# Images 19 to 31 of an iterated matrix square root: the square is turned by VectorE and DMAs, where TensorE transposed v

## The chip, the cores and the metric

The kernel runs on one core of a Trainium2 chip. The metric is the device time of one execution in microseconds (us). TensorE (PE in the profile; its weight loads are PEld) multiplies matrices from SBUF into PSUM. VectorE (DVE) and ScalarE (ACT) read and write PSUM and SBUF; GpSimd (POOL) works on SBUF alone. SyncE (SP) computes nothing and issues DMAs; ACT can issue DMAs too. Each engine takes its instructions in order.

## The reference

Input x is 32 images of 32 channels of 128x128 float32. Layer 0 adds to each channel the approximate square root of its normalised self:

```
x = x + _L0_conv_ref(_gn(x))         # _gn: mean and variance over pairs of channels
  # _L0_conv_ref, for each of the 1024 matrices A2 (128x128):
  normA = jnp.sqrt(jnp.sum(A2 * A2, axis=(1, 2)))
  Y = A2 / normA;  Z = I
  for _ in range(5):
      T = 0.5 * (3.0 * I - jnp.matmul(Z, Y))
      Y = jnp.matmul(Y, T)
      Z = jnp.matmul(T, Z)
  sA = Y * jnp.sqrt(normA)
x = x + _L1_conv_ref(_gn(x), weights1, weights2)
  # a 2-D Fourier transform of each channel, 2 x 32 x 32 low modes multiplied by a
  # 32x32 channel matrix each, and the transform back
```

## The kernel before

**Tiles.** The work of layer 0 is cut into 256 groups of four channels (8 groups to an image). A group's tiles are 128 partitions by 4 x 128 float32 (256 KB). `products(lhsT, rhs)` is four matmuls into one PSUM bank, `lhsT` transposed times `rhs` for each channel; TensorE records two instructions for each float32 product of 128 columns, and one for a transpose. `m` holds the matrices in one orientation, `mb` (loaded as `b`) in the other, since `lhsT` must come transposed.

**One group** is one call of `newton` (line 462). Five steps of the iteration are folded into two polynomials of degree four ("quartics") and a last step. There are two forms. Images 1 to 18 are "far" (`is_far`, line 357): `far_quartic` (line 442). Image 0 and images 19 to 31 are "near": `near_quartic` (line 407). The near form:

- TensorE makes the square, `products(mb, m)`; VectorE adds a multiple of m from SBUF and writes `v`.
- GpSimd makes `r = mb + eye` (a 128x512 TENSOR_TENSOR).
- TensorE transposes `v` (four transposes through PSUM); VectorE adds `r` and writes `w`.
- TensorE makes `products(v, w)`; VectorE adds the scaled identity and writes `q`.

The second quartic of a group runs on a new `m` (ScalarE's copy of a product) and on `mb`, its transpose, which TensorE makes and ScalarE copies (`taken(transposed(m), "mb", more)`).

The far form has no such transposes. VectorE turns the square block by block straight out of PSUM (`turned`, 32x32 blocks within each set of 32 partitions); two DMAs on the sync engine carry the result to DRAM (`away`) and back in another order of blocks (`back`), and `by_rows` reads it as the transposed square.

**Staging.** Before a group starts, `fetch` (line 366) loads its two inputs, and `staged` (line 375) normalises them. In near groups GpSimd does all four channels of `m` (four 128x128 TENSOR_SCALAR) and ScalarE the four of `mb`. In far groups ScalarE does two of the four of `m`, and GpSimd also makes a first `v` from `eye_v - mb`. The loads of far groups are issued by the sync engine, those of near groups by ScalarE.

**Order.** The program is written out by hand, as generators. In each "round" every group under way (a "lane") does one step, up to its next `yield`; `rest` is two yields. A near group starts every five rounds (`NEAR = 25 / 5`), a far group every three. A near group lives for some 22 rounds, so that four to five are in flight. Between the lanes' steps the loop at line 1115 places the steps of everything else: statistics of coming images (`prep`), the tail of a finished group (`settle`: store to DRAM, folds on GpSimd, statistics), the forward transform, the mode products and the inverse transform (`inverse`, line 953). The inverse of images 0 to 19 runs beside the groups of the later images. It loads `yt` and `ob` and stores `out` on the sync engine (512 KB each for yt and out) and has GpSimd add `d` to `yt`. Engines and queues keep exactly this order. The transfers that SP and ACT issue take eight semaphores in turn, so that each waits until the one that last used its semaphore has landed.

**Buffers.** `rooms` (line 308) gives the tags of four-channel tiles their numbers of buffers: the first number lasts for the whole run, the second is for `early` tiles, which are there only until `MORE` groups are done.

Of the kernel before, what the change touches and what calls it, by code (L numbers as in the profile page):

```python
# [36 lines left out]
P = 128  # L37
# [56 lines left out]
def conv_preact_kernel(  # L94
# [127 lines left out]
    def prep(bs, made):  # L222

        n = len(bs)
        nc_, ng = n * C, n * G
        first_b = bs[0]
        st = small.tile([P, ng, 6], F32, tag="a_st", name=f"a_st{first_b}", bufs=2)
        tiles = []
        parts = [(b, i) for b in bs for i in range(C // 4)]

        ahead = 3 if first_b else 8

        def load(k):
# [12 lines left out]
        for k in range(len(parts)):  # L246
            for j in range(2):
                nc.vector.bn_stats(st[:, 2 * k + j, :], tiles[k][:, j, :])
            yield
            if k + ahead < len(parts):  # L250
                load(k + ahead)
        ms = small.tile([P, ng], F32, tag="a_ms", name=f"a_ms{first_b}")
        nm, d = yield from moments(st, ms, "a")
        yield from pause
        pq = bank()[:, 0, 0:nc_]
        nc.tensor.matmul(pq, avg_mean, d.rearrange("p g c -> p (g c)"), start=True, stop=True)
        if not first_b:
# [26 lines left out]
        off = off.rearrange("p g c -> p (g c)")  # L284
        sn = small.tile([P, nc_], F32, tag="a_t_s", name=f"a_t_s{first_b}", bufs=3)
        for k, b in enumerate(bs):
            g, c = slice(k * G, k * G + G), slice(k * C, k * C + C)
            made[b] = (nm[:, g], sc[:, c], off[:, c], sn[:, c])
        yield
        nn = small.tile([P, ng, 2], F32, tag="a_d", name=f"a_n{first_b}")  # L290
        nc.vector.tensor_tensor(
            nn,
            s[:, 0:nc_].rearrange("p (g c) -> p g c", c=2),
            iv[:, nc_:, None].to_broadcast([P, ng, 2]),
            ALU.mult,
        )
        nn = nn.rearrange("p g c -> p (g c)")
        for far in sorted({is_far(b) for b in bs}):
            of = [k for k, b in enumerate(bs) if is_far(b) == far]
            c = slice(of[0] * C, of[-1] * C + C)  # L300
            f = EYE_Q * QS if far else EYE * QF
            nc.vector.tensor_scalar_mul(nn[:, c], nn[:, c], P * (1.5 / f) ** 2)
        yield
        yield from root(nn, nc_, sn)
        yield


    rooms = dict(b=(4, 6), xt=(10, 5), x=(3, 2), r=(4, 0), v=(3, 2), w=(3, 2), q=(4, 2))
    rooms.update(my=(4, 3), mb=(2, 4), t=(3, 2), y4=(2, 2), turn=(0, 4))
    turns = dict.fromkeys(rooms, 0)  # L310

    def four(tag, more):
# [8 lines left out]
    def taken(ps, tag, more, f=1.0):  # L321
        t = four(tag, more)
        if f == 1.0:
            nc.scalar.copy(t, ps)
        else:
            nc.scalar.mul(t, ps, f)
        return t
# [12 lines left out]
    def minus(eye, m, t):  # L340

        nc.gpsimd.tensor_tensor(t, eye, m, ALU.subtract)
        return t
# [13 lines left out]
    def is_far(b):  # L357
        return 0 < b < FIRST

    def has_more(b, g):  # L360

        return b * (C // 4) + g < MORE
# [1 line left out]
    raw = {}  # L364

    def fetch(b, g):
        queue = nc.sync if is_far(b) else nc.scalar
        xt, t = four("xt", has_more(b, g)), four("b", has_more(b, g))
        kept(queue.dma_start(out=t, in_=x[b, :, 4 * g : 4 * g + 4, :]))
        kept(queue.dma_start(out=xt, in_=xt_in[b, :, 4 * g : 4 * g + 4, :]))  # L370
        raw[b, g] = xt, t
# [3 lines left out]
    def staged(b, g, nm, sc, off, sn):  # L375

        m = four("x", has_more(b, g))
        xt, mb = raw.pop((b, g))

        def on_scalar(t, x, offset, scale, c):  # L380
            c = slice(c, c + 1)
            kept(
                nc.scalar.activation(t, x, AF.Identity, bias=offset[:, c], scale=scale[:, c])
            )

        for j in range(4):
            c = 4 * g + j
            if j < 2 or not is_far(b):
                kept(
                    nc.gpsimd.tensor_scalar(  # L390
                        m[:, j, :],
                        xt[:, j, :],
                        nm[:, c // 2 : c // 2 + 1],
                        sc[:, c : c + 1],
                        ALU.add,
                        ALU.mult,
                    )
                )
            else:
                on_scalar(m[:, j, :], xt[:, j, :], off, sc, c)  # L400
            on_scalar(mb[:, j, :], mb[:, j, :], off, sc, c)
            yield
        v = minus(eye_v, mb, four("v", True)) if is_far(b) else None
        ready.append((xt, m, mb, v))
        yield

# [32 lines left out]
    def by_rows(t):  # L439
        return blocks(t).rearrange("p a c j -> p c a j")  # L440

    def far_quartic(m, mb, v, f, later, more):

        ps = products(m, mb)
        held = away(turned(ps, more))
        if later:
            yield
        nc.vector.scalar_tensor_tensor(v, ps, 1 / (9 * MS), v, ALU.mult, ALU.add)
        if not later:
            yield  # L450
        minus(eye_q, m, m)
        yield
        w = back(held, "w", more)
        yield
        yield from rest
        q = plus(products(v, by_rows(w)), 9 / (39 * MS**2 * f**2), m, "q", more)
        yield from rest
        return q

    rest = (None, None)  # L460

    def newton(g, sn, xt, m, mb, v, far, more):


        qf, et, eye_t = (QS, EYE_Q, eye_q) if far else (QF, EYE, eye)
        if far:
            q = yield from far_quartic(m, mb, v, 1.0, False, more)
        else:
            q = yield from near_quartic(m, mb, more)
        my = four("my", more)  # L470
# [23 lines left out]
        else:  # L494
            nc.scalar.mul(m, ps, MS / qf)
            yield from rest
            mb = taken(transposed(m), "mb", more)
            yield from rest
            q = yield from near_quartic(m, mb, more)
            both = [bank().rearrange("p (j k) x -> p j k x", k=2) for _ in range(2)]  # L500
            for j in range(4):
                nc.tensor.matmul(both[j // 2][:, j % 2], q[:, j], my[:, j], start=True, stop=True)
# [612 lines left out]
    while todo or any(lanes) or posts or specs or prods or backs:  # L1115
# [3 lines left out]
        for i in range(LANES):  # L1119
# [5 lines left out]
            if lanes[i] is None and todo and room and rounds >= due:  # L1125
                due = max(due, rounds - 1) + (FAR if far else NEAR)
                while norms:
                    step(norms)
                b, g = todo.pop(0)
                xt = ready[0][0]  # L1130
                lanes[i] = (b, g, xt, newton(g, made[b][3], *ready.pop(0), far, has_more(b, g)))
                if stages:
                    stage()
                if not todo:
                    loads.append(weights())
# [88 lines left out]
```

## Time and profile before

| | |
|---|---|
| median of 3 runs | 2981.98 us (2980.7 to 2986.93) |
| profiled execution: time, span | 2981.79 us, 2980.0 us |
| mean granted TensorE clock in it | 0.988 |
| TensorE matmul / weight load busy | 2849.7 us (96%) / 2663.8 us (89%) |
| VectorE / ScalarE / GpSimd busy | 77% / 52% / 67% |
| DMA | 711.90 MB, mean 239 GB/s |

The span runs from the first instruction to the last. A line of the costliest groups names the engine and the operation, the tile written and those read, their shapes, the count, the busy time and the mean of one, and then the engine's idle time just before these instructions with what ended it. A row of a table by stage gives, for a stretch of the span, its length, then the busy time (and count) of PE, PEld, DVE, ACT and POOL, the granted clock, the mean share of time in which the 16 DMA engines were busy, and GB/s. All instructions carry line 88, where a helper records them, so tiles tell them apart. Far groups run from about 30 us to 1560 us, near groups of images 19 to 31 from 1541 us to 2912 us.

### The profile page before, as it was taken

The page shows a single profiled execution, that of the slowest core. Times are in us where ns is not written, and L with a number is a line of the kernel's source. Part 1 is how long each engine was busy: PE and PEld are TensorE (multiplying, and loading weights), DVE is VectorE, ACT ScalarE, POOL GpSimd, SP SyncE. Part 2 cuts the span into 40 slices and gives each one's busy share as a digit, 9 for nine tenths or more (in the row PEclk, how much of TensorE's full clock was granted, in tenths as well). Part 3 has the DMA queues.
Part 4 walks back from the last instruction along what each step waited for, and adds up shares of the span by engine and source line. Part 5 has one row for each costly group of instructions (what it writes and reads, how often), then busy time and mean ns, then how long its engine had stood idle before and what let it go on. Part 6 is the DMA issues. An engine that isn't in the chain of part 4 may idle for free.

```text
span 2980.0 us, 73661 instructions
## 1 busy us (share of the span) xinstructions
PE 2849.7 (96%) x27688; PEld 2663.8 (89%) x27688; DVE 2285.7 (77%) x4407; ACT 1541.3 (52%) x3899; POOL 1988.4 (67%) x2308
## 2 busy tenths in 40 slices
PE   7999999999999999999999999999999999999995
PEld 7899999999999899999999888888888899888983
DVE  7878898889788888888876545886876876777665
ACT  4555555555555555555544445545555544655452
POOL 4667767777777767767755534777777763678452
PEclk9999999999999999999999999999999999999997
DMA  5688889888888889898943566867877737666567
GB/s 177 199 280 272 253 267 281 275 266 282 269 275 257 283 253 294 253 291 255 303 139 104 157 203 208 284 231 242 281 242 248 261 124 226 209 230 218 186 211 268
DMA packets 566897, 711.90 MB, mean 239 GB/s; under 512 B 94736, under 2 KB 329232, under 8 KB 566544
## 3 DMA queue, kind: packets, MB, share of 16 engines
q1 hardware_dynamic: 494400, 574.26, 59.9%
q10 hardware_dynamic: 72144, 132.94, 13.7%
q8 instruction: 221, 3.62, 0.5%
q14 instruction: 132, 1.08, 0.1%
HBM read 440.17 MB, written 266.86 MB: 237 GB/s over the span
## 4 chain that ended last, share of the span: by engine, by line
PE 72%; DMA 12%; DVE 9%; issue 2%; POOL 2%; ACT 1%; SPq 1%; ACTq 0%; DVEq 0%; POOLq 0%
PE ps L88 72%; DMA xs<-in_xs 3%; DMA w<-turn 3%; DVE yt L88 1%; DVE turn L88 1%; DMA turn<-turn 1%; DVE b_d L88 1%; DMA yt<-mid 1%; DMA ob<-od 1%; DVE a_st L88 1%; DVE root L88 1%; DVE q L88 1%; DVE b_st L88 1%; SPq L88 1%; DVE v L88 1%
## 5 line engine op out<-in xcount | busy, mean ns | idle before, releaser
L88 POOL TENSOR_TENSOR fold<-xt 128x256 f32<-128x256 f32 x512 | 364.1, 734 | 308.4 <-DVE xt L88 274.2
L88 ACT ACTIVATE b<-b,a_off,a_sc 128x128 f32<-128x128 f32 x1024 | 467.2, 492 | 127.2 <-issue 27.9
L88 ACT ACTIVATE my<-ps 128x512 f32<-128x512 f32 x512 | 302.4, 602 | 410.4 <-PE ps L88 278.0
L88 PE MATMUL ps<-my,q 128*128 128x128 f32 (+1 forms) x2944 | 475.9, 309 | 6.5 <-ACT my L88 6.4
L88 POOL TENSOR_TENSOR yt<-yt,d 128x512 f32<-128x512 f32 x244 | 306.6, 1283 | 212.3 <-ACT d L88 192.8
L88 PEld LDWEIGHTS ps<-my,q 128*128 128x128 f32 x2944 | 411.9, 191 | 35.4 <-ACT my L88 7.6
L88 PE MATMUL ps<-w,v 128*128 128x128 f32 x2944 | 399.2, 279 | 26.1 <-DMA w<-turn 11.9
L88 POOL TENSOR_TENSOR v<-eye_v,b 128x512 f32<-128x512 f32 x144 | 184.0, 1278 | 352.2 <-ACT b L88 316.2
L88 ACT ACTIVATE t<-ps 128x256 f32<-128x256 f32 (+1 forms) x368 | 171.1, 467 | 462.8 <-PE ps L88 447.2
L88 PEld LDWEIGHTS ps<-w,v 128*128 128x128 f32 x2944 | 362.2, 193 | 41.7 <-issue 10.5
L88 POOL TENSOR_SCALAR x<-xt,a_nm,a_sc 128x128 f32<-128x128 f32 x736 | 323.7, 456 | 15.3 <-DVE a_sc L88 15.0
L88 DVE STREAM_TRANSPOSE turn<-ps 128x512 f32<-128x512 f32 x432 | 295.4, 698 | 45.3 <-PE ps L88 36.9
L88 ACT ACTIVATE y<-ps,a_t_s 128x128 f32<-128x128 f32 x1024 | 292.2, 372 | 42.9 <-PE ps L88 42.7
L88 PE MATMUL ps<-q,t 128*128 128x128 f32 x2048 | 273.4, 277 | 1.3 <-DVE r L88 1.3
L88 PEld LDWEIGHTS ps<-q,t 128*128 128x128 f32 x2048 | 249.0, 192 | 4.2 <-DVE r L88 1.5
L88 DVE BATCH_NORM_STATS2 a_st<-xs 128x6 f32<-128x256 f32 x504 | 184.9, 409 | 77.9 <-DMA xs<-in_xs 77.5
L88 DVE SCALAR_TENSOR_TENSOR w<-ps,r 128x512 f32<-128x512 f32 x224 | 152.9, 683 | 108.7 <-PE ps L88 75.3
L88 DVE SCALAR_TENSOR_TENSOR q<-ps,eye 128x512 f32<-128x512 f32 x224 | 153.3, 684 | 94.2 <-PE ps L88 90.1
L88 DVE TENSOR_TENSOR xt<-ps,xt 128x512 f32<-128x512 f32 x256 | 174.4, 681 | 50.6 <-PE ps L88 48.2
L88 POOL TENSOR_TENSOR r<-mb,eye 128x512 f32<-128x512 f32 x112 | 143.1, 1278 | 86.3 <-ACT mb L88 86.3
L88 DVE TENSOR_TENSOR yt<-ps,yt 128x512 f32<-128x512 f32 x256 | 163.0, 681 | 46.5 <-PE ps L88 40.9
L88 DVE BATCH_NORM_STATS2 b_st<-xt 128x6 f32<-128x256 f32 x512 | 188.0, 407 | 0.5
(147 smaller groups left out, 6296.5 us busy)
## 6 DMA issues: line engine op xcount, KB each, us to landing
turn<-turn SPq DMA_DIRECT2D x432, 256.0 KB
w<-turn SPq DMA_DIRECT2D x288, 256.0 KB
mid<-xt SPq DMA_DIRECT2D x256, 256.0 KB
yt<-mid SPq DMA_DIRECT2D x128, 512.0 KB
xs<-in_xs ACTq DMA_DIRECT2D x252, 256.0 KB
out<-yt SPq DMA_DIRECT2D x115, 512.0 KB
b<-in_x SPq DMA_DIRECT2D x144, 256.0 KB
xt<-in_xt SPq DMA_DIRECT2D x144, 256.0 KB
```

The source lines that it names most:

```text
L88: return self.tc.keep_in_program_order(issue(*args, **kw))
```

## The change

It concerns images 19 to 31 ("late": `b >= FIRST`, 104 groups, 208 quartics).

- `late_quartic` takes the place of `near_quartic`. The square `products(mb, m)` is turned out of PSUM by VectorE (`turned`, as in the far form). `across` then moves it straight to another SBUF tile `w` by four DMAs on the sync engine: each takes 32 partitions and writes 128 partitions by 128 columns (64 KB in pieces of 512 bytes). VectorE adds the square to a `v` that already holds `eye_v - m`. GpSimd turns `mb` into `eye_q - mb` in place. The second product is `products(v, by_rows(w))`, and VectorE adds the new `mb`. The transposes of `v` on TensorE, `r = mb + eye` and the addition of `r` are gone.
- The yields of the new quartic stand at the same distances as in the near one: the second product comes four steps after the first.
- For late groups GpSimd makes `eye_v - m`, once in `staged` (tag `v`) and once in `newton` (tag `r`), and two of the four channels of `m` in `staged` go to ScalarE.
- The loads of late groups (`fetch`) are issued by the sync engine. Image 0 stays on ScalarE.
- `rooms` is dealt anew: `q` 3 and 3 (4 and 2 before), `t` 2 and 3 (3 and 2), `turn` 2 and 2 (0 and 4).
- The scale factors follow (`prep`, `newton`).

```diff
-    rooms = dict(b=(4, 6), xt=(10, 5), x=(3, 2), r=(4, 0), v=(3, 2), w=(3, 2), q=(4, 2))
-    rooms.update(my=(4, 3), mb=(2, 4), t=(3, 2), y4=(2, 2), turn=(0, 4))
+    rooms = dict(b=(4, 6), xt=(10, 5), x=(3, 2), r=(4, 0), v=(3, 2), w=(3, 2), q=(3, 3))
+    rooms.update(my=(4, 3), mb=(2, 4), t=(2, 3), y4=(2, 2), turn=(2, 2))
...
+    def is_late(b):
+        return b >= FIRST
...
-        queue = nc.sync if is_far(b) else nc.scalar
+        queue = nc.sync if b else nc.scalar
...
-            if j < 2 or not is_far(b):
+            if j < 2 or not b:
...
-        v = minus(eye_v, mb, four("v", True)) if is_far(b) else None
+        v = minus(eye_v, mb if is_far(b) else m, four("v", has_more(b, g))) if b else None
...
+    def across(t, more):
+
+        w = four("w", more)
+        for a in range(4):
+            src = t[32 * a : 32 * a + 32].rearrange("p c x -> p (c x)")
+            kept(
+                nc.sync.dma_start(
+                    out=w.rearrange("p c x -> p (c x)")[:, P * a : P * a + P],
+                    in_=src.rearrange("p (b x) -> p b x", b=4),
+                )
+            )
+        return w
+
+    def late_quartic(m, mb, v, more):
+
+        ps = products(mb, m)
+        w = across(turned(ps, more), more)
+        nc.vector.scalar_tensor_tensor(v, ps, 1 / (9 * MS), v, ALU.mult, ALU.add)
+        yield
+        minus(eye_q, mb, mb)
+        yield
+        yield from rest
+        q = plus(products(v, by_rows(w)), 9 / (39 * MS**2), mb, "q", more)
+        yield from rest
+        return q
...
+        elif late:
+            q = yield from late_quartic(m, mb, v, more)
...
             mb = taken(transposed(m), "mb", more)
+            v = minus(eye_v, m, four("r", more)) if late else None
             yield from rest
-            q = yield from near_quartic(m, mb, more)
+            if late:
+                q = yield from late_quartic(m, mb, v, more)
+            else:
+                q = yield from near_quartic(m, mb, more)
```

More of the change, by code (lines that the diff above doesn't have):

```diff
@@ L297, in prep @@
         nn = nn.rearrange("p g c -> p (g c)")
[L298 to L302, printed above, removed]
+        f = EYE_Q * QS if first_b else EYE * QF
+        nc.vector.tensor_scalar_mul(nn, nn, P * (1.5 / f) ** 2)
         yield
@@ L460, in conv_preact_kernel, with newton @@
     rest = (None, None)
-    def newton(g, sn, xt, m, mb, v, far, more):
-        qf, et, eye_t = (QS, EYE_Q, eye_q) if far else (QF, EYE, eye)
+    def newton(g, sn, xt, m, mb, v, far, late, more):
+        qf, et, eye_t = (QS, EYE_Q, eye_q) if far or late else (QF, EYE, eye)
         if far:
             q = yield from far_quartic(m, mb, v, 1.0, False, more)
+        elif late:
+            q = yield from late_quartic(m, mb, v, more)
         else:
@@ L1130, in conv_preact_kernel @@
                 xt = ready[0][0]
-                lanes[i] = (b, g, xt, newton(g, made[b][3], *ready.pop(0), far, has_more(b, g)))
+                lanes[i] = (b, g, xt, newton(g, made[b][3], *ready.pop(0), far, is_late(b), has_more(b, g)))
                 if stages:
```

## The prediction

> **What bounds the kernel now.** I read the page's busy times and slices first: does one engine carry the whole span, or stages in turn?
>
> ```profile
> PE 2849.7 (96%) x27688; PEld 2663.8 (89%) x27688; DVE 2285.7 (77%) x4407; ACT 1541.3 (52%) x3899; POOL 1988.4 (67%) x2308
> PE   7999999999999999999999999999999999999995
> POOL 4667767777777767767755534777777763678452
> DMA  5688889888888889898943566867877737666567
> PE ps L88 72%; DMA xs<-in_xs 3%; DMA w<-turn 3%; DVE yt L88 1%; DVE turn L88 1%; DMA turn<-turn 1%; DVE b_d L88 1%; DMA yt<-mid 1%; DMA ob<-od 1%; DVE a_st L88 1%; DVE root L88 1%; DVE q L88 1%; DVE b_st L88 1%; SPq L88 1%; DVE v L88 1%
> ```
>
> TensorE bounds it from end to end, and the chain that ends last is PE for 72%. The change touches the last stage of groups alone, so I split that by what runs beside it (columns: stretch, length, busy PE, PEld, DVE, ACT, POOL, clock, DMA share, GB/s).
>
> ```profile
> 200.00:1400.00 1200.00, 1172.17 (x10611) 1132.57 (x10611) 1020.15 (x2002) 647.16 (x1662) 881.32 (x976) 1.00 0.86 272
> 1541.00:1700.00 159.00, 154.23 (x1405) 145.83 (x1407) 100.86 (x204) 74.95 (x190) 81.35 (x112) 0.99 0.37 116
> 1700.00:1890.00 190.00, 182.27 (x2161) 163.33 (x2152) 104.58 (x202) 91.05 (x222) 84.89 (x111) 1.00 0.69 218
> 1890.00:2400.00 510.00, 489.19 (x4330) 441.83 (x4330) 399.45 (x734) 267.12 (x703) 398.05 (x458) 0.99 0.73 250
> 2600.00:2720.00 120.00, 116.10 (x1020) 105.17 (x1013) 89.93 (x155) 71.60 (x168) 95.03 (x109) 0.97 0.71 236
> ```
>
> The first row is far groups, which turn by VectorE and DMA already: PE 98% busy with the DMA engines at 0.86. In the late stretches PE is busy 1319.7 of 1371 us. From 1890 to 2400 and from 2600 to 2720 the inverse runs beside the groups, and GpSimd stands at 78% and 79%; elsewhere it is at 45 to 57%. The prices come from the groups by form in 1541 to 2912:
>
> ```profile
> L88 POOL TENSOR_SCALAR x<-xt,a_nm,a_sc 128x128 f32<-128x128 f32 x396 | 172.9, 457 | 0.0
> L88 DVE SCALAR_TENSOR_TENSOR w<-ps,r 128x512 f32<-128x512 f32 x204 | 139.4, 683 | 105.0 <-PE ps L88 72.8 <-POOL r L88 19.7 <-POOL x L88 10.7
> L88 POOL TENSOR_TENSOR r<-mb,eye 128x512 f32<-128x512 f32 x103 | 131.6, 1277 | 72.4 <-ACT mb L88 72.4
> L88 PE MATMUL ps<-ident,v 128*128 128x128 f32 x816 | 126.3, 278 | 5.2 <-DVE v L88 2.6 <-DVE b_mq L88 2.5
> ```
>
> and from TensorE's order of time, where starts can be subtracted, and the waits of PE among far groups:
>
> ```profile
> 2026.78 0.60 PE L88 MATMUL ps<-ident,v 128*128 128x128 f32 x4
> 2027.21 0.60 PE L88 MATMUL ps<-ident,my 128*128 128x128 f32 x4
> 2027.65 1.06 PE L88 MATMUL ps<-x,b 128*128 128x128 f32 x8
> ```
> ```profile
> PE ps L88 <- DMA w<-turn: 15.7, 16, 3.2
> ```
>
> **Transposes of v.** 104 groups x 2 quartics x 4 = 832 leave TensorE. Their duration, 278 ns, is that of overlapping work; what one takes from the next is start to start, (2027.21 - 2026.78)/4 = 0.109 us. Nothing else can use that time in a stretch where PE is the bound: 832 x 0.109 = 91 us. The other end is the row's busy time, 126.3/816 x 832 = 129 us, too high because neighbouring groups share it. I take -91. The products that stay cost the same: far products that read through `by_rows` (w and v, four pieces of 32 columns) start 112 ns apart in the trace, like the plain ones.
>
> **The turned square's way to TensorE.** This is a new wait, and the order gives it four rounds. PE stands in order behind it: if `w` is late, `products(v, by_rows(w))` holds up the four other groups and the inverse. I measured the room in the trace of before. In 1890 to 2400 VectorE starts on the square 1.8 us (median) after its first matmul; at the same place it would now run the block transpose (0.70 us; 698 ns in the page). From the end of that to the products that read `w` there are 8.8 us at the median, 7.8 at the lower quartile, 6.0 in the lowest twentieth; fewer transposes between take some 0.7 us off. In that room go four issues (0.37 us each on SP, as `w<-turn` of far groups) and the landing. The nearest transfer there is `mid<-xt`, same queue, 256 KB: by its packets it ends 3.0 us after its issue at the median, 6.1 at the upper quartile, 6.8 in the worst tenth, since 512 KB loads and stores stand ahead of it. So the last of the four, issued 1.2 us after the block transpose, lands after 4 to 5 us of 8.1 usually, and after about 8 in the worst tenth. One set in six or so comes late, by 1 to 1.5 us: 0.2 us per set. SP itself is no obstacle in before: its last DMA ahead of each set's place had gone out before the block transpose would end, but for 0.3 us in a few stretches. Low end: far groups, 15.7 us over 122 groups x 2 sets = 0.064 us per set, or 13 us for 208 sets. High end: 0.9 us per set, 190 us, if landings move by 3 us because the shared queue holds eight more transfers per group and each DMA waits for the one eight before it. Between them I take 0.19 us per set, +40 us, nearer to far groups, whose DMA engines are busier (0.86) than these will be.
>
> That last number: q1's price in far groups is 77.3% of 16 x 1200 us for 291.6 MB, 50.9 engine-us per MB. A set of 0.262 MB takes 13.3/16 = 0.83 us of all engines; 208 sets 173 us, 13 points on the 0.65 of 1541 to 2912, and 0.73 becomes about 0.88 where it is densest.
>
> The Trainium skill has a rule against this change (SBUF — State Buffer, "Door 1: The DMA port swizzle"): a block of 32 partitions reaches 8 of 16 ports, with 189 GB/s measured, and transfers on different blocks do not make up for each other. By it I estimate 4 x 65.5 KB / 189 GB/s = 1.39 us for a set, landing 0.55 us later; with some 0.1 us more wait per set the sum would be 21 us higher. The trace does not show that surcharge: in 1700 to 1890, where 104 of q1's transfers are 64 KB pieces into 32 partitions (`diag<-in_wk`), q1 took 52.4% of 16 x 190 us for 31.32 MB, again 50.9 engine-us per MB. I keep to the row.
>
> **GpSimd.** Per group it loses two TENSOR_SCALAR (2 x 0.457) and gains two TENSOR_TENSOR (2 x 1.277: `v` in `staged`, `r` in `newton`); the two `r = mb + eye` become two `eye_q - mb`. Net +1.64 us per group. From 1890 to 2400 there are 39 groups (156 TENSOR_SCALAR / 4): 398 + 64 = 462 us of work, against 510 - 39 x 0.87 = 476 us that PE would need. 97% full, in order, it becomes a second bound there and in 2600 to 2720 (9 groups: 95 + 15 = 110 of 112). Elsewhere 45 to 57% leaves cover. Who waits if it lags: VectorE's `q` (three rounds after `eye_q - mb`), the second `v` (two rounds), and SP at the `out` stores, with the sets queued behind them. Low end 0. High end: the 112 us that GpSimd idles in 1890 to 2400 all stay: 462 + 112 - 476 = +98. Since 104 of these 112 us are waits of `yt` for ScalarE's `d`, that is GpSimd running ahead, I stay near the low end: 0.25 us for each of 48 groups, +12.
>
> **ScalarE** gains two 0.486 us ACTIVATEs per group (101 us in 1371, where it is busy 708) and loses two DMA issues. In before it stood with `my` behind its own DMA issues 31 us (12.7 + 7.6 + 7.3 + 3.4, by the releasers of its waits), and PE waited for `my` 18.8 us. Some of that goes: 0 to -19, I take -5.
>
> **At nothing.** VectorE: a transpose of 0.70 and two additions for three additions of 0.68, +0.03 us per group, under its 20 to 45% idle time. SP: eight issues and two loads, 3.8 us per group of 13; hidden by its idle time, and if not, it is part of the set's wait. `rooms` keeps all totals, so far groups see no fewer buffers; late quartics hold two of three `q`, `w` and two `turn` in turns, free a round or more before reuse. PSUM: two banks per quartic in place of three. The stretch after 2912 stays.
>
> **Sum.** -91 + 40 + 12 - 5 = -44 on the profiled execution's 2981.79 us (span 2980.0), which is the median of the runs, 2981.98, within 0.2 us: 2938 us. All low ends give 2982 - 129 + 13 - 19 = 2847, all high ends 2982 - 91 + 190 + 98 = 3179.
>
> **Rivals.** *Sets come late (slower).* In 1890 to 2400 bursts of two `out`, two `yt` and two `ob`, 2.5 MB, go out every 26 us on the same queue; a set behind one waits for it. Against it: the median room of 3 us, and far groups. For it: far groups have three rounds of 3.3 us (1200 us / 122 groups / 3) for one transfer of 256 KB with no such bursts beside. It decides above (91 - 12 + 5)/208 = 0.40 us per set. At 1 us for the 96 sets beside the inverse and 0.4 us for the other 112, 141 us: 2982 - 91 + 141 + 12 - 5 = 3039 us. Chance 0.35.
> *GpSimd sets the pace beside the inverse.* The 48 groups gain nothing but the sets' waits are covered: 60 us for GpSimd's term and 25 for the sets: 2982 - 91 + 60 + 25 - 5 = 2971. Chance 0.12.
> *No late sets,* at far groups' price: 2982 - 91 + 13 - 10 = 2894. Chance 0.12.
> *The transposes stood in time that PE would have waited anyway* (it is idle 51 of 1371 us, and VectorE's `w` and `q` wait for PE, not the reverse, which speaks against it): about 2980. Chance 0.04.
>
> **Numbers.** The forecast has 0.37. About 0.2% is what a measurement here tells from no change. Faster: forecast, no late sets, and most of GpSimd's case, 0.58; same 0.06; slower 0.36. The range from 2885 to 3025 leaves out a few hundredths below and the larger half of the slow rival's own spread above, about 0.17. Where the faster cases hold, 2885 to 2975 is theirs.
>
> **What would show it.** PE's `ident,v` gone, PE instructions fewer by 832, group starts in 1890 to 2400 12 to 13 us apart in place of 13.1. Sets late: PE waiting for `w` by DMA in the list of waits, over 84 us in total, at stretches with `out` and `yt`. GpSimd: its share over 92% in 1890 to 2400 with VectorE's `q` or `v` waiting for POOL. The forecast is wrong if the landings on the shared queue are several microseconds longer than `mid` shows, or if SP, now filled, stands behind an `out` store whose GpSimd addition is late.

## The result, and the profile after

The changed kernel is slower: 3061.2 us (median, 3055.63 to 3072.24) against 2981.34 us (2979.65 to 2986.93) for the kernel before on the same chip. The ratio is 1.0265, with a 95% interval of 1.0243 to 1.0287. The forecast was 2938 us, with 2885 to 3025 as its range and 0.36 for slower. The profiled execution took 3061.83 us, span 3060.0 us, mean granted clock 0.975 (before 0.988).

First the page of the changed kernel: busy times, slices of PE and of the DMA engines, and the chain that ended last by line.

```profile
PE 2796.3 (91%) x26856; PEld 2602.0 (85%) x26856; DVE 2276.4 (74%) x4406; ACT 1607.8 (53%) x4107; POOL 2155.7 (70%) x2308
PE   7999999999999999999999889898998888898985
DMA  5698889898888888888756668888989667797786
PE ps L88 51%; DMA w<-turn 7%; SPq L88 6%; DMA yt<-mid 4%; DMA xs<-in_xs 3%; DMA xt<-in_xt 2%; DVE turn L88 2%; DMA turn<-turn 2%; DVE yt L88 1%; POOL yt L88 1%; DMA b<-in_x 1%; DVE q L88 1%; DMA plain<-in_wk 1%; DVE a_st L88 1%; DVE b_d L88 1%
```

PE has 832 instructions fewer, as worked out, and is no longer filled: from slice 23 on its row is full of eights. Its share of the chain fell from 72% to 51%, and two entries that were at 3% and 1% stand at 7% (`w` by DMA) and 6% (SPq, the sync engine's own issuing). No engine took PE's place as the bound by its busy time; the time went into waits. By stage (the columns are those of the table before: stretch, length, PE, PEld, DVE, ACT, POOL, clock, DMA share, GB/s), cut near the same groups, to within some 20 us; 2640 to 2770 is left out:

```profile
1541.00:1715.00 174.00, 161.89 (x1516) 150.39 (x1518) 110.95 (x221) 93.83 (x240) 112.20 (x122) 0.98 0.60 175
1715.00:1920.00 205.00, 176.85 (x1977) 158.27 (x1969) 109.66 (x217) 99.64 (x249) 111.73 (x118) 0.96 0.76 233
1920.00:2440.00 520.00, 460.35 (x3961) 412.28 (x3960) 384.13 (x717) 285.62 (x765) 450.13 (x447) 0.97 0.86 278
2440.00:2640.00 200.00, 171.37 (x2243) 157.64 (x2241) 119.01 (x233) 98.75 (x241) 107.07 (x115) 0.93 0.69 199
2770.00:2988.00 218.00, 184.35 (x2427) 166.15 (x2428) 130.49 (x232) 113.42 (x274) 142.24 (x144) 0.95 0.76 228
```

From 1541 us to the last group PE was idle 51 of 1371 us before, and is idle 177 of 1447 us now. So its idle time rose by 126 us and its busy time fell by 50, which makes the +76 of this stage. The fall is 41 short of the 91 us of transposes, and the clock says where most of that went: the column has 0.97 to 1.00 before and 0.93 to 0.98 now. In this trace's record of the clock it stands at 0.50 for 113 us of the stage, 92 of them with PE busy; before it was 26 us, 21 of them busy. If PE does half the work in such a time (eight matmuls below took 2.04 us in it for 1.06), its work counted at full clock fell by estimate from 1309 to 1223 us, that is by 86, and the low clock cost 36 us more than before. So 126 us of idle time, 36 us of low clock and 86 us of work gone make the +76.

Where the loss falls is seen from the starts of the same group in both traces. Counted from the end, group 85 starts at 1745.5 us before and at 1745.4 after; group 77 at 1861.4 and 1874.6; group 37 at 2399.5 and 2429.1; group 21 at 2601.0 and 2661.7; group 13 at 2711.7 and 2772.4; the last product of the last group at 2912.0 and 2988.0. So 13 us are lost in 8 groups beside the mode products of the first images (1700 to 1890 before), 16 us in the 40 groups beside the inverse, 31 us in 16 groups beside the next mode products, and 15 us in the last 13. The prediction looked for the loss beside the inverse; per group, it is four to five times greater beside the mode products.

What SP does there. Its waits from 1575 to 2900 us (who is waited for: us in all, times, longest), first before:

```profile
SPq L88 <- DVE xt L88: 269.0, 41, 13.3
SPq L88 <- POOL yt L88: 147.5, 56, 4.7
SPq L88 <- PE ps L88: 104.0, 61, 6.0
SPq L88 <- DMA yt<-mid: 93.4, 42, 6.0
```

and after:

```profile
SPq L88 <- DVE r L88: 81.7, 43, 7.9
SPq L88 <- DMA yt<-mid: 76.5, 79, 2.7
SPq L88 <- DVE v L88: 42.8, 35, 6.4
SPq L88 <- DVE q L88: 26.7, 32, 3.1
```

Before, SP stood for long in front of a DMA whose data VectorE, GpSimd or PE had not made yet: it was early. Now these waits are small, and the largest that are left, on VectorE's `r` and `v`, are nearly all in front of a move: they end with the block transpose of the set, as the first move starts 0.03 us behind it. Adding up SP's own DMA instructions between 1575 us and the last group shows why: 754 instructions, 351 of 1337 us (0.26) before; 1737 instructions, 1011 of 1413 us (0.72) after. In the same stretch its waits for an engine, which are its slack, fell from 731 to 250 us, and those for the landing of a DMA from 232 to 156. The moves have this row (count, then minimum, median and maximum in ns, first and last start):

```profile
L88 SPq DMA_DIRECT2D w<-turn x753: 542/602/1902, 1574.8 to 2895.3; - x189
```

A move takes SP 0.602 us at the median, where the prediction put 0.37. SP's old DMAs take longer too: some 750 that both kernels have rose from 349 to 416 us. `mid<-xt`, the same transfer in both, took 0.32 us at the median before and takes 0.59 now, when 89 of 102 start less than 0.1 us behind another DMA. And who suffers from a late SP is seen in PE's waits from 1545 to 2980 us:

```profile
PE ps L88 <- DMA w<-turn: 96.9, 47, 9.2
PE ps L88 <- DMA plain<-xs: 24.1, 9, 5.6
PE ps L88 <- DMA diag<-xs: 13.0, 2, 7.9
PEld ps L88 <- DMA w<-turn: 10.5, 4, 5.3
PEld ps L88 <- POOL fold L88: 8.5, 4, 5.8
PE ps L88 <- DMA diag<-in_wk: 5.5, 5, 2.5
```

Besides `w`, the inputs of the mode products (`plain`, `diag`), which SP issues too, come late: 46.5 us over PE and PEld together, where it was 14.6 before.

One place, in SP's order of time (start, us, what was issued) and in PE's:

```profile
2511.46 0.36 SPq L88 DMA_DIRECT2D b<-in_x  x1
2515.66 0.33 SPq L88 DMA_DIRECT2D xt<-in_xt  x1
2516.10 4.58 SPq L88 DMA_DIRECT2D w<-turn  x4
2520.78 0.53 SPq L88 DMA_DIRECT2D plain<-in_wk  x1
2521.36 1.84 SPq L88 DMA_DIRECT2D diag<-xs  x4
2523.30 0.37 SPq L88 DMA_DIRECT2D plain<-in_wk  x1
2523.77 2.92 SPq L88 DMA_DIRECT2D od<-om  x4
2526.78 5.12 SPq L88 DMA_DIRECT2D w<-turn  x4
```

```profile
2504.79 1.06 PE L88 MATMUL ps<-w,v 128*128 128x128 f32 x8
...
2522.43 2.04 PE L88 MATMUL ps<-w,v 128*128 128x128 f32 x8 [5.72 <-DMA w<-turn]
...
2533.72 1.13 PE L88 MATMUL ps<-w,r 128*128 128x128 f32 x8 [3.46 <-DMA w<-turn]
```

The load of `xt` stands 3.8 us until a load that ScalarE issued at 2511.32 us (`xs<-in_xs`) has landed, which used the same semaphore. The four moves stand behind it and take 4.6 us, 2.2 of them a wait for another such load, and ten more DMAs without a pause separate them from the next set. PE waits 5.72 us for the first set and 3.46 us for the second. After the first wait the same eight matmuls take 2.04 us where they took 1.06: the granted clock is 0.50 from 2521.5 to 2528.3 us. After the shorter wait they take 1.13, but the clock falls then too, just after they end, from 2535.1 to 2538.5 us. So a gap costs more than its length. The Trainium skill (TensorE: Matmul & The Clock Gate, "Part 1: The HAM clock gate (the "warmup" mystery)") has the clock fall to half once PE has been idle for a window of about 3.4 us. The length agrees: these two stretches of half clock are 6.8 and 3.4 us long. That PE must be idle for the whole window does not, and here the measurement decides: after 1500 us full clock ended 26 times in this trace, each time behind 3.41 us in which PE was busy for less than 0.47 of the time, and only 7 of the 26 behind 3.41 us with next to no work (under 0.02).

### The profile page after: what moved, and what is told of

It reads as the page before. It is cut to its first block, busy times and chain, and to the rows that moved or that the text cites. A ratio compares the mean times of both kernels' runs of the same rounds, so it can differ in the third digit from the quotient of the medians.

```text
span 3060.0 us, 73947 instructions
## 1 busy us (share of the span) xinstructions
PE 2796.3 (91%) x26856; PEld 2602.0 (85%) x26856; DVE 2276.4 (74%) x4406; ACT 1607.8 (53%) x4107; POOL 2155.7 (70%) x2308
## 4 chain that ended last, share of the span: by engine, by line
PE 51%; DMA 23%; DVE 11%; SPq 6%; issue 3%; POOL 3%; ACT 2%; ACTq 0%; DVEq 0%; POOLq 0%
PE ps L88 51%; DMA w<-turn 7%; SPq L88 6%; DMA yt<-mid 4%; DMA xs<-in_xs 3%; DMA xt<-in_xt 2%; DVE turn L88 2%; DMA turn<-turn 2%; DVE yt L88 1%; POOL yt L88 1%; DMA b<-in_x 1%; DVE q L88 1%; DMA plain<-in_wk 1%; DVE a_st L88 1%; DVE b_d L88 1%
## 5 line engine op out<-in xcount | busy, mean ns | idle before, releaser
L88 DVE STREAM_TRANSPOSE turn<-ps 128x512 f32<-128x512 f32 x640 | 443.6, 702 | 137.4 <-PE ps L88 101.2
L88 ACT ACTIVATE b<-b,a_off,a_sc 128x128 f32<-128x128 f32 x1024 | 484.0, 494 | 71.8 <-DMA turn<-turn 20.0
L88 PE MATMUL ps<-w,v 128*128 128x128 f32 x2112 | 295.1, 284 | 94.3 <-DMA w<-turn 79.2
L88 PEld LDWEIGHTS ps<-w,v 128*128 128x128 f32 x2112 | 266.3, 197 | 114.0 <-issue 52.2
L88 PE MATMUL ps<-w,r 128*128 128x128 f32 x1984 | 270.4, 280 | 38.7 <-DMA w<-turn 35.4
L88 POOL TENSOR_TENSOR v<-eye_v,x 128x512 f32<-128x512 f32 x104 | 132.5, 1274 | 229.0 <-ACT x L88 204.9
L88 PEld LDWEIGHTS ps<-w,r 128*128 128x128 f32 x1984 | 244.4, 194 | 48.9 <-issue 33.9
L88 ACT ACTIVATE x<-xt,a_off,a_sc 128x128 f32<-128x128 f32 x496 | 244.5, 493 | 3.1 <-DMA turn<-turn 1.5
L88 POOL TENSOR_SCALAR x<-xt,a_nm,a_sc 128x128 f32<-128x128 f32 x528 | 232.6, 451 | 16.3 <-DVE a_sc L88 15.7
L88 DVE SCALAR_TENSOR_TENSOR q<-ps,b 128x512 f32<-128x512 f32 x104 | 71.4, 687 | 211.4 <-PE ps L88 193.3
```

The lines of the kernel that those rows point to most:

```text
L88: return self.tc.keep_in_program_order(issue(*args, **kw))
```

## The experiments

All times are medians beside the kernel before on the same chip, and ratios have 95% intervals. Edits are against the changed kernel unless said. The theory at the start was the prediction's first rival (late sets, PE waiting for `w`); against it stood SP's time, the bytes, and GpSimd. In the expectations A is late sets from a full SP queue, B GpSimd, C the added traffic of the DMA engines, and Q, which came after e1 to e4, the full queue by itself.

**The wait for `w` taken away, the moves kept; and the moves taken away.**

```diff
-        w = across(turned(ps, more), more)
+        t = turned(ps, more)
+        across(t, more)                      # e2_no_dma: this line goes too
...
-        q = plus(products(v, by_rows(w)), 9 / (39 * MS**2), mb, "q", more)
+        q = plus(products(v, by_rows(t)), 9 / (39 * MS**2), mb, "q", more)
```

> The second product of late quartics reads the tile that VectorE turned (SBUF) in place of w; all four DMAs of each set are still issued and land in w, which nobody reads. What is left out: the moves between partitions do not reach the product, so the output is not the reference's. Theory A (SP's queue: four issues of 0.60 us per set, in order with the loads and the product transfers, bring w late, and PE's clock falls with the idle time): PE's wait for w (97 us after 1541 us) goes, the granted clock returns towards 0.985, the waits for diag and plain (37 us) stay: 2910 to 2970 us. Theory B (GpSimd's extra 1.64 us per group sets the pace): 3030 or more. Theory C (the landing itself is slow from the extra DMA traffic): like A here.

> As e1_no_wait, but the 832 moves are not issued at all (left out: the moves; the output is not the reference's). Theory A: SP is as free as before, 2880 to 2910 us, and 30 us or more below e1 since diag, plain and xs loads are no longer behind the sets. Theory B: still 2990 or more. Theory C: like A, but e1 and e2 within 15 us of each other, because landing alone was the trouble.

Measured: e1 3040.57 us, 1.0204 (1.0173 to 1.0234); e2 2933.03 us, 0.9843 (0.9812 to 0.9873). A had foretold 2910 to 2970 us for e1. With no product waiting for `w` at all, only about 20 us come back. Some 107 us hang on 832 DMAs that nobody reads. This refutes the first rival as the main cause. SP's DMA instructions fill 0.73 of the stage in e1, 0.34 in e2. (e2 stays above the 2880 to 2910 us of A; GpSimd, below, is the reason that was found.) In e1 PE's waits turn to other work:

```profile
PE ps L88 <- DVE t L88: 28.2, 11, 9.5
PE ps L88 <- DMA plain<-xs: 25.0, 11, 5.7
PEld ps L88 <- POOL fold L88: 21.1, 8, 5.8
PE ps L88 <- DMA plain<-in_wk: 16.2, 4, 7.1
PEld ps L88 <- DMA plain<-in_wk: 14.7, 3, 7.4
```

**The loads back on ScalarE, and one round more for the set.**

```diff
-        queue = nc.sync if b else nc.scalar
+        queue = nc.sync if is_far(b) else nc.scalar      # e3_loads_on_act
...
         minus(eye_q, mb, mb)
         yield
+        yield                                            # e4_round_more
         yield from rest
```

> The late groups' input loads are issued by ScalarE again, as in before; the rest is the changed kernel. Theory A: SP gets 0.9 us of issue per group back and the loads no longer stand ahead of a set: 20 to 50 us faster than the changed kernel (3010 to 3040). Theory B and C: no difference beyond 10 us, or slower since ScalarE stands behind its own issues again.

> One more yield ahead of the second product of each late quartic: w has five rounds instead of four, some 2.7 us more, and a group lives two rounds longer. Theory A and C: the direct wait of PE for w falls from 97 us to under 40, with the clock's share 60 to 90 us faster than the changed kernel, 2970 to 3000. Theory B: within 10 us of the changed kernel.

Measured: e3 3089.61 us, 1.0368 (1.0332 to 1.0404); e4 3118.11 us, 1.0446 (1.0409 to 1.0482). Both are slower than the change, where A had foretold both faster. In e3 PE waits less for `w` (71.5 us for 96.9), but ScalarE stands in order behind its own loads: its waits for landings are 76 us, 34 in the changed kernel. So moving the loads to SP was the better half of the change. In e4 the wait for `w` falls too, to 69.4 us, and the kernel loses 57 us more; ScalarE's wait for the product `my` is 269.9 us there (161.6 in the changed kernel). Longer groups for the same four or five in flight may be behind that; it was not tried apart and stays open. It shows again that the wait for `w` is not the price.

**Bytes, pieces or DMAs?** Nobody reads `w` in these four, as in e1.

```diff
-        for a in range(4):
-            src = t[32 * a : 32 * a + 32].rearrange("p c x -> p (c x)")
-            nc.sync.dma_start(
-                    out=w.rearrange("p c x -> p (c x)")[:, P * a : P * a + P],
-                    in_=src.rearrange("p (b x) -> p b x", b=4),
+        nc.sync.dma_start(out=w, in_=t)                          # e7_one_issue, e10 (kept(...) around each left out)
+        for a in range(3):                                       # e10_one_and_three_tiny alone
+            nc.sync.dma_start(out=spare[a][:, 0:4], in_=t[0:16, a, 0:4])
...
+                    out=w.rearrange("p c x -> p (c x)")[:, P * a : P * a + 8],    # e8_few_bytes
+                    in_=src.rearrange("p (b x) -> p b x", b=4)[:, :, 0:8],
...
+            nc.sync.dma_start(out=w[rows], in_=t[rows])          # e9_four_plain, four times 32 partitions
```

> As e1_no_wait (nobody reads w; the moves do not reach the product, so the output is not the reference's), but each set is one DMA of the same 256 KB from partition to the same partition: one issue, one semaphore, packets of 2 KB. Theory Q: nearly all of the 107 us between e1 (3041) and e2 (2933) goes, 2935 to 2960. Theory C: most of it stays, 3000 or more.

> As e1_no_wait, but each of the four moves of a set carries 8 of 128 columns (pieces of 32 bytes, a sixteenth of the bytes; the rest is left out, and the output is not the reference's). Issues, semaphores and descriptors stay. Theory Q: within 20 us of e1, 3020 to 3060. Theory C: near e2, 2935 to 2960.

> As e1_no_wait, but the four DMAs of a set copy 32 partitions each to the same partitions, in pieces of 2 KB (the move between partitions is left out, the output is not the reference's): four issues and four semaphores, a quarter of the descriptors. If SP's issue time counts (0.60 us each for the moves, some 0.33 us for such a plain one): halfway, 2970 to 3005. If the number of DMAs, each waiting for the one eight before, counts: within 15 us of e1, 3025 to 3055. Theory C: within 15 us of e1 as well, but then e7 too.

> As e7_one_issue (2951; nobody reads w, the output is not the reference's), with three more DMAs of 16 partitions by 16 bytes per set: four issues and four semaphores, next to no bytes or descriptors. If the number of DMAs on SP counts, by issue time or by semaphores, it comes up to e8 (3022) or e1 (3041): 3000 to 3060. If the cost lies in the moves' many small pieces: within 15 us of 2951.

| | DMAs per set | KB per set | us | ratio | SP's share on DMAs | SP on DMAs + for landings, us |
|---|---|---|---|---|---|---|
| e2 | 0 | 0 | 2933.03 | 0.9843 (0.9812 to 0.9873) | 0.34 | 444 + 118 |
| e7 | 1 | 256 | 2950.92 | 0.9900 (0.9863 to 0.9937) | 0.45 | 579 + 144 |
| e8 | 4 | 16 | 3022.11 | 1.0139 (1.0105 to 1.0173) | 0.73 | 1009 + 149 |
| e1 | 4 | 256 | 3040.57 | 1.0204 (1.0173 to 1.0234) | 0.73 | 1021 + 160 |
| e9 | 4 | 256 | 3071.47 | 1.0304 (1.0264 to 1.0345) | 0.69 | 988 + 236 |
| e10 | 1 + 3 tiny | 257 | 3070.16 | 1.0276 (1.0214 to 1.0339) | 0.69 | 978 + 272 |

SP's share is the time of its DMA instructions from 1575 us to the last group; the last column has that time and what SP stood in front of its instructions until some DMA had landed. The time goes with the number of DMAs, not with their bytes. All 256 KB in one DMA cost 18 us; a sixteenth of the bytes in four DMAs saves only 19 us on e1; three DMAs of 256 bytes beside the one large cost 112 us by the ratios. Larger pieces do not help: e9 moves pieces of 2 KB in place of 512 bytes and is 30 us slower than e1. SP's share alone does not order the four with four DMAs: e9 and e10, at 0.69, are slower than e8 and e1, at 0.73. The sums of the last column go with the times: 562, 723, 1158, 1181, 1224 and 1250 us from e2 to e10, and in the profiled executions the late groups take longer in the same order. That speaks for a wait for a landing at the head of SP's queue costing as much as an issue; it was not tried apart. Why e9 and e10 wait longer for landings, no run gives. A tiny DMA out of SBUF into SBUF takes SP as long as a move:

```profile
L88 SPq DMA_DIRECT2D w<-turn x186: 504/517/1412, 1575.3 to 2894.1; - x186
L88 SPq DMA_DIRECT2D spare<-turn x558: 507/582/2333, 1576.0 to 2897.0; - x186
```

(both of e10: one of 128 partitions, three of 16 partitions by 16 bytes). The Trainium skill (DMA: Bandwidth & Descriptors, "Issuing engines are not separate DMA queues") says that the time a sequencer takes to initiate a DMA "is usually small relative to the DMA itself". Set against the 2.7 us from a move's issue to its last packet (median, below), 0.60 us of SP is small here too. But it is three times the 0.21 us that by the prediction's price a move takes of the 16 engines, and all of these issues went through one in-order issuer.

**The idle DMAs put into the kernel before.** If DMAs on SP are the cause, they must slow the kernel before too, where nothing else of the change is made.

```diff
     def near_quartic(m, mb, more, late=False):      # against the kernel before
...
+        if late:
+            for a in range(4):
+                kept(nc.sync.dma_start(out=aside[a], in_=v[32 * a : 32 * a + 32, :, 0:8]))   # e12: SBUF to SBUF
+                kept(nc.sync.dma_start(out=aside[a], in_=v[:, a, 0:8]))                      # e16: SBUF to DRAM, in its place
+        # e15: e12's four in four successive steps
```

> The kernel before, with four idle DMAs on SP added to each quartic of images 19 to 31: 32 partitions each, 128 bytes per partition, from v to a tile that nobody reads; nothing else of the change. Theory Q: these 832 issues alone slow the kernel before by 50 to 110 us, 3030 to 3090. If the change's cost lies in w itself, in GpSimd or in the loads on SP: within 15 us of 2981.

> As e12_before_plus_issues (3096: the kernel before and 832 idle issues on SP), but the four idle DMAs of a quartic stand in four successive steps in place of one behind the other. Number of DMAs and turns on the eight semaphores are the same. If back-to-back issue time (0.59 us each) on SP is the cost, single issues take 0.33 to 0.45 us and 30 to 60 us of the 110 go: 3035 to 3065. If the turns on the semaphores are the cost, each idle DMA still has to wait for the one eight before it: within 15 us of 3096, or slower.

> As e12_before_plus_issues (3096), but the four idle DMAs of a quartic go from v (128 partitions, 32 bytes each) to a few DRAM bytes that nobody reads, in place of 32-partition pieces between tiles. Same number, same places, same turns on the semaphores; SP's stores to DRAM took 0.32 to 0.45 us to issue in before, against 0.59 us. If SP's issue time is the cost: 30 us or more of e12's 110 go, 3030 to 3065. If the number of turns counts: within 15 us of 3096.

Measured: e12 3096.35 us, 1.0364 (1.0313 to 1.0415); e15 3133.52 us, 1.0492 (1.0444 to 1.0540); e16 3059.3 us, 1.0237 (1.0207 to 1.0267). The rows of e12 and e16, with minimum, median and maximum in ns:

```profile
L88 SPq DMA_DIRECT2D aside<-v x731: 585/592/2218, 1577.2 to 2899.9; - x183
```

```profile
L88 SPq DMA_DIRECT2D aside<-v x762: 319/384/1863, 1574.8 to 2899.1; - x191
```

832 idle DMAs alone cost the kernel before 107 us, as much as they cost between e2 and e1. With the same count but 0.384 in place of 0.592 us of SP each, 69 us: the costs stand as 0.64 to 1, the issue times as 0.65 to 1, and SP's shares are 0.54 and 0.66. That speaks for SP's time as the main price. It does not settle it alone. With SP's waits for landings the sums are 958 + 289 us in e12 and 769 + 366 in e16, against 350 + 232 before. Where the eight semaphores are shared in turn, ScalarE's loads wait for transfers that they have no business with; in e12 this row is new (of ScalarE's waits):

```profile
ACT b L88 <- DMA aside<-v: 62.8, 25, 6.6
```

All of ScalarE's waits for landings come to 159 us in e12 and 99 in e16, against 46 before, and SP's own waits for the idle transfers are 138.3 us in e16 and 111.5 in e12. How much of the 107 us is SP's own time and how much the turn of the semaphores stays open. e15 was to tell whether four in a row are worse than four apart; the issues did not become shorter (0.591 us), and VectorE now waited 70.9 us to overwrite a `v` that a later step still read, so its extra cost says nothing of that.

**Other ways for the square.**

```diff
-                nc.sync.dma_start(
+                (nc.scalar if a % 2 else nc.sync).dma_start(      # e6_two_queues
...
-        w = across(turned(ps, more), more)
+        held = away(turned(ps, more))                             # e5_via_dram
...
         minus(eye_q, mb, mb)
         yield
+        w = back(held, "w", more)
```

> Two of the four moves of each set are issued by ScalarE, two by SP; everything else is the changed kernel. Number of DMAs, semaphores and bytes stay; SP's issue time falls by 1.2 us per set. If SP's issue time is what counts: 20 us or more faster than the changed kernel's 3061, less what ScalarE loses. If the number of transfers in turn on eight semaphores counts: no faster, and slower by the issue time on ScalarE and its wait for VectorE's block transpose, 3080 to 3150.

> The turned square goes to DRAM and back as in the far form (two DMAs per set on SP, one after the other, the second issued one step later) in place of four moves between tiles. Same result. Theory Q (SP's queue is full: 2.4 us of issue and four of the eight semaphores per set): two issues of 0.35 us and two semaphores, while the landing takes longer, so 2950 to 3000 us. Theory C (extra traffic of the DMA engines): twice the bytes per set, so slower than the changed kernel, 3080 or more. Theory of late landings alone: two landings in a row, 5 us against 4.8, so within 20 us of 3061.

Measured: e6 3124.9 us, 1.0459 (1.0408 to 1.0511); e5 3295.39 us, 1.1045 (1.1008 to 1.1083). If SP's issues were the price, 2950 to 3000 us was foretold for e5 and a gain of 20 us or more, less ScalarE's loss, for e6. In e6 SP falls to 0.49 and PE's wait for `w` to 40.6 us, but ScalarE, which has work of its own, now stands in order before a DMA whose source VectorE has not turned (`ACT b <- DVE t`, 108.6 us in all; the other case foretold, the semaphores in turn with this wait, had 3080 to 3150 us). In e5 SP has half the moves, but the second of each pair waits at the head of SP's queue until the first has landed, with everything else behind it (waits of 1575 to 2900 us):

```profile
SPq L88 <- DMA turn<-turn: 491.4, 140, 8.6
PE ps L88 <- DMA w<-turn: 188.8, 72, 6.7
```

So the number of DMAs is not the only thing that holds SP; a wait in front of one does it as well.

**GpSimd by itself, and half the change.** e13 is e2 without `minus(eye_q, mb, mb)` (VectorE adds `mb` as it is). e14 makes only the first quartic of a group the new way, with the factors of the old for the second.

```diff
-        minus(eye_q, mb, mb)                                  # e13_no_dma_less_pool
...
-            v = minus(eye_v, m, four("r", more)) if late else None
-            if late: q = yield from late_quartic(m, mb, v, more)
+            q = yield from near_quartic(m, mb, more)          # e14_first_only
...
```

> As e2_no_dma (2933, no moves), and GpSimd does not make eye_q - mb (left out: VectorE adds mb as it is; the output is not the reference's): 2.55 us less GpSimd work per group, 0.9 us less than in the kernel before. If GpSimd's lag is what keeps e2 at -49 us where the transposes are worth -91 (in e2 PE waits some 49 us for fold): 2885 to 2905. If not: within 10 us of 2933.

> Only the first quartic of each late group has the new form, the second is as in before (same result, half the sets: four moves and 4 transposes fewer per group, the loads on SP). By the parts measured so far: transposes -46 us, GpSimd some +10 (it gains 0.36 us per group net), 416 issues at half of the 107 to 119 us that 832 cost, or less if SP's cost grows with its fill: 0 to +20 us against before, 2980 to 3000. If the cost of the issues were only that of sets being late, it would be 2950.

Measured: e13 2893.65 us, 0.9685 (0.9600 to 0.9771); e14 2995.41 us, 1.0034 (1.0016 to 1.0052). e13 is the change with neither the moves nor GpSimd's second addition. From it to e2 the ratios differ by 47 us, with 25 us of uncertainty from e13's interval. What PE waits for agrees with it. In e2, then in e13:

```profile
PEld ps L88 <- POOL fold L88: 28.5, 10, 5.8
PE ps L88 <- POOL fold L88: 20.9, 9, 4.4
```

```profile
PEld ps L88 <- POOL fold L88: 3.3, 1, 3.3
```

With half the moves (SP at 0.53), e14 just fails to break even. None of these kernels that does the whole work beats the kernel before.

## Why the prediction was wrong

Put together from the ratios, each times 2981.3 us: e13 -94; e13 to e2 (GpSimd) +47; e2 to e7 (the bytes in one DMA) +17; e7 to e1 (three more DMAs per set) +91; e1 to the change (the wait for `w` itself) +18. Sum +79. The late groups alone, from the first product of group 104 to the last of group 1 in the profiled executions, give -89, +39, +21, +87 and +17. Each step is priced in this order; in another order it could cost more or less.

- **The step that failed** is the one under "At nothing": "SP: eight issues and two loads, 3.8 us per group of 13; hidden by its idle time, and if not, it is part of the set's wait." Each half is wrong. The issues took 0.60 us, not the 0.37 of far groups, where one DMA comes back from DRAM into 128 partitions; here 32 partitions go from SBUF to SBUF, and the prediction carried the price over without saying that it was a bound. With the loads (medians 0.38 and 0.45) that is 8 x 0.60 + 0.83 = 5.6 us per group, and the DMAs behind them took longer as well. And it is no part of the set's wait alone: SP's instructions for the mode products, the stores and loads of the inverse and the inputs of coming groups are in the same queue, and they were all pushed back. That was the largest term, 91 us for three of four DMAs, and its price in the sum was zero.
- **Why idle time was no cover.** The prediction asked whether SP's last DMA ahead of a set had gone out in before, and found that it had. It had, because SP was early. But SP's idle time is in front of a DMA whose data is late; a DMA that comes 3 us later moves what is behind it too, and the queue need not be full for that: 0.72 on the mean was enough, as 0.54 in e16 was for 69 us. The prediction's own sign for a filled SP, that it stands behind an `out` store whose GpSimd addition is late, is not what happened: SP's waits for `yt` of GpSimd fell from 147.5 to 12.7 us.
- **The wait for `w`**: +40 for 0.19 us per set. PE did wait 107 us for it (96.9 + 10.5), 0.52 us per set, over the bound of 84 us that the prediction gave as the sign of the slow rival. But of this only 18 to 20 us is its own cost, since without it PE waits elsewhere for the same late SP (e1). The rival "sets come late" named 3039 us and the right side, not the right cause.
- **The landing** by itself was no worse than forecast, by 76 sets of 1920 to 2440 us whose packets can be told apart. From the last issue to the last packet it took 2.7 us at the median and 3.5 at the upper quartile, where `mid` had 3.0 and 6.1. Yet from the end of the block transpose the whole set took 7.0 us, 8.6 at the upper quartile and 9.8 at the worst tenth, for 4 to 5 and 8: the first issue came 1.0 us late (2.5 at the upper quartile), and the four took 2.9 us for 1.5. SP again. The DMA engines' share there is 0.86, about the 0.88 worked out.
- **The transposes**, -91: e13 gives -88 against the usual median of before and -95 against that of its own runs, with a little less GpSimd work than before as well. The gap of starts was the right price, within the 25 us of e13's interval (the two printed starts give 0.1075 us; the median of such transposes in this stage is 0.109). In the changed kernel PE's busy time fell by only 50 us, with some 36 us of low clock against it.
- **GpSimd**, +12: the step from e13 to e2 measured +47 (some 20 to 74). It takes 2.55 us of GpSimd work per group, the term was for 1.64, so what the term should have been is not measured alone; but the lower end was the wrong one to stay near. It was not seen at the share foretold (87% of 1920 to 2440, not over 92%), nor in VectorE's `q` and `v`: it was `fold`, which PE waits for in order. That follower was not in the prediction's list. In the changed kernel PE and PEld wait only 10.7 us for it, because SP holds PE up first.
- **ScalarE**, -5 from loads taken off it: the sign agrees with e3, where putting them back costs 28 us. But that is the price with a full SP, not the one foretold.
- **The rule on ports** that the prediction cites and sets aside: its row was weak evidence, since the 104 transfers are 6.8 of the 31.3 MB there. But e8, with a sixteenth of the bytes from and to the same partitions, gains only 19 us on e1. So the path of the bytes was rightly not the main matter, and the count of DMAs, which neither the rule nor the row spoke of, was.
- **Group distance**: 12 to 13 us foretold beside the inverse; it is (2429.1 - 1874.6)/40 = 13.9.

Open: the split between SP's time and the semaphores in turn, the reason why e4 got slower than the change, and why e9 and e10 wait longer for landings than e1.

## What to carry to other kernels

Count the DMAs that a change adds to an issuing engine's queue, price them by a row with the same source, destination and number of partitions and with another DMA right in front, and add them to that engine's time like any compute instruction. Well before the sum fills a stage (here 0.45 cost 17 us more than 0.34 in e7, and 0.54 cost 69 us in e16) everything in that queue may be late, not only the new transfers. Add the time that the engine stands until a DMA has landed; its waits for data that an engine has yet to make are the slack. An engine's idle time covers additional work only if what stands behind it in order has slack too: ask of each follower when it is needed, and by whom. When one wait is taken out of a profile to see what it costs, compare the time and not the wait: here 107 us of waiting for `w` were worth 20.

## What the runs showed of the hardware

- SP's time for one DMA hardly went by its bytes; it went by its ends and by what stood in front, at the median. From SBUF to SBUF in 16 or 32 partitions it was 0.51 to 0.59 us after a pause of SP of over 1.5 us and 0.59 to 0.60 less than 0.1 us behind another DMA (256 bytes in e10 as 64 KB in the changed kernel); 128 partitions from SBUF to SBUF 0.47 to 0.52 (e7, e10); 128 partitions to DRAM 0.32 after a pause and 0.43 behind another (e16); 32 partitions from DRAM (`diag<-in_wk`) 0.31 and 0.42.
- DMAs that nobody reads slow a kernel: 832 of them on SP, 69 us at 0.384 us each and 107 us at 0.592.
- Transfers issued by one engine hold up another engine's loads with which they share only the turn of the semaphores: ScalarE's waits for landings rose from 46 to 159 us in e12.
- After a gap of 5.7 us eight PE matmuls took 2.04 us at a granted clock of 0.50, where they take 1.06. After a gap of 3.5 us they took 1.13, and the clock fell to 0.50 1.4 us after work had begun again. The granted clock of the stages with gaps was 0.93 to 0.98.
- Half clock did not need an idle PE: over the traces of all 17 kernels full clock ended 447 times after 1500 us, 426 times behind 3.41 us in which PE was busy for less than half the time; 5625 other stretches of 3.41 us left the clock full, and in all but 62 of them PE was busy for at least half.
